# mLSTM stage: eight heads' scores in four PSUM banks at once, gates on four column groups, and the state's product ahead of the scores

## The chip, the cores and the metric

The kernel runs on one core of one Trainium2 chip. Its time is the device time in microseconds, and the number to compare is the median of several executions: 733.33 us here, over three (732.94 to 734.95). One further execution was recorded by the hardware profiler; it took 733.4 us, of which the span from the first to the last instruction is 731.6 us. Every duration below comes from that execution. TensorE (PE) multiplies matrices into PSUM, its weight loads are shown apart as PEld, VectorE is DVE, ScalarE is ACT, GpSimd is POOL, and SyncE (SP) issues most DMAs.

## The reference, cut to what matters

Two transformer-like layers follow each other on x of 4 x 256 tokens with 256 features, in float32: an attention, a gated feed-forward with a Hadamard transform, an mLSTM block with its own gated feed-forward, and a feed-forward with int8 weights. A layer norm stands after each. The part that the change touches is the mLSTM, with 8 heads of 16 query and key features and 32 value features:

```
i = cap(h @ w_ig + b_ig); f = cap(h @ w_fg + b_fg)      # two gates per head and token, cap = 15*tanh(x/15)
F = cumsum(log_sigmoid(f)); D[s,t] = F[s] - F[t] + i[t]  for t <= s, else -inf
m = max_t D;  C = (q k^T / 4) * exp(D - m)
out = (C @ v) / max(|sum_t C|, exp(-m)), then a norm per head, and sigmoid(o) times it
x1 = x + out @ w_out ;  then rmsnorm and silu(x1 w_gate) * (x1 w_up) @ w_down
```

The kernel splits a sequence of 256 tokens in two blocks of 128. Within a block it forms the scores directly; the second block gets what the first one left from a state, the sum of k v^T over the first block, multiplied by q.

## The kernel before

The tokens are cut in two halves `n` = 0 and 1, each of 512 tokens, which are two sequences `bb`. After the attention (to about 434 us) the feed-forward of half 0 runs, then the mLSTM of half 0 while the feed-forward of half 1 (`ffn0(1)`) fills in, then the feed-forward that belongs to the mLSTM (`ffn1(0)`), and with it the mLSTM of half 1; then `ffn1(1)` and the int8 feed-forward.

`mlstm(n)` is a Python generator. Each number that it yields is a wait in microseconds that its author reckons with; `merge(first, other)` (L958) advances the filling stream by about that much matmul work before it goes on. The filling stream yields 1.7 after each of its 512-column products in `glu` (L543) and after each half of a `down` product (L557). This makes the program's order; the build then fixes one order of instructions for each engine, which may move an instruction ahead of others that have to wait. Each engine works through its own list in that order.

For one half the steps are: `mlstm_in` (L613) normalizes the tokens, transposes them to `fm` (L534), multiplies by `w_if` for the gates, by `w_qk` for q and k (L639 f.), and by `w_vo` for v and the output gate, four times (L651). `gates` (L674) is a chain of small ACT and DVE steps on the gate values, which lie on 64 partitions; its running maximum `gmax` goes to DRAM as `far` (L689). `by_token` (L699) transposes three rows of factors to token order (`tok`), and the keys are multiplied out once more by token (`ks`). `within` (L736) handles four heads of one sequence: it loads `far` back, broadcast over 128 partitions, as `wide` (L740), multiplies q and k of four heads in two PSUM banks (L747), subtracts `wide` from a mask on POOL (L756), takes eight exponentials on ACT (L763), and multiplies scores and exponentials on DVE (L767). `between` (L711) forms the state (L714, L719) and its product with q (L726, L729). `attend` (L773) multiplies by the values (L778), one small product per head and block. `head_norm` (L788) is a chain on DVE and ACT that ends in `xs` (L808). Then follow the transposes of `xs` (L534), `w_out` (L850), the addition to `acc` (L851), and in `ffn1` a root mean square norm (L517 to 527), transposes of `h` (L534) and the first product with `w_gate`.

[...] The mLSTM takes its banks in turn from two pairs (`pt`, `ot`), the filling stream from the other two pairs (`mm`, `sc`).

A float32 matmul stands in the trace as two MATMUL records with a weight load each; counts in the profile are therefore twice those in the code. [...]

Of the kernel before, what the change touches and what calls it, by code (L numbers as in the profile page):

```python
# [16 lines left out]
P = 128  # L17
# [21 lines left out]
def tile_two_layers(ctx: ExitStack, tc: tile.TileContext, a: dict, out: bass.AP):  # L39
# [26 lines left out]
    def mm_k(ps, lhs, rhs, n):  # L66

        for i in range(n):
            nc.tensor.matmul(ps, lhsT=lhs(i), rhs=rhs(i), start=(i == 0), stop=(i == n - 1))  # L69


    wts = tc.alloc_tile_pool(name="wts", bufs=1, side="right")
# [394 lines left out]
    w_if = late.tile([P, KC, 64], F32, tag="w_if", name="w_if")  # L467
    nc.gpsimd.memset(w_if, 0.0)
    nc.sync.dma_start(w_if[:, :, 0:40], a["w_if"])
    b_if = late.tile([64, 2], F32, tag="b_if", name="b_if")  # L470
    nc.gpsimd.memset(b_if, 0.0)
    for bb in range(2):
        for g in range(2):
            nc.sync.dma_start(b_if[32 * bb : 32 * bb + H1, g : g + 1], a["b_if"][32 * g : 32 * g + H1, :])
    vecs = load("vecs", [P, 6])
    w_vo = load("w_vo", [P, KC, 2 * D])
    w_qk = late.tile([P, KC, 2, P], F32, tag="w_qk", name="w_qk")
# [51 lines left out]
    def transposed(src, dst, tag, weight=None):  # L529
# [10 lines left out]
                evicted = nc.vector.tensor_scalar(dst[:, c, :], pt, weight[:, c : c + 1], None, ALU.mult)  # L540
        return evicted

    def glu(xT, wg, wu, hT, tag):  # L543

        for c in range(NH):
            cols = slice(c * P, (c + 1) * P)
            pg, pu = bank(tag), bank(tag)
            mm_k(pg, lambda i: wg[:, i, cols], lambda i: xT[:, i, :], KC)
            yield 1.7
            mm_k(pu, lambda i: wu[:, i, cols], lambda i: xT[:, i, :], KC)  # L550
            g = work.tile([P, HALF], F32, tag="glu_g", name="glu_g")
            nc.scalar.activation(g, pg, AF.Tanh, scale=0.5)
            nc.vector.scalar_tensor_tensor(g, g, 1.0, pg, ALU.add, ALU.mult)
            nc.vector.tensor_tensor(hT[:, c, :], pu, g, ALU.mult)
            yield 1.7
# [45 lines left out]

    ones = mix.tile([2 * 32, S], F32, tag="ones", name="ones")
    nc.gpsimd.memset(ones, 1.0)
    bias = mix.tile([2 * 32, 2], F32, tag="bias", name="bias")
    nc.scalar.mul(bias, b_if, 1.0 / CAP)
    DV = DV1 + 1
    HV = H1 * DV
# [5 lines left out]
    def mlstm_in(n, t):  # L613
# [5 lines left out]
        transposed(hin, fm, "m", vecs[:, 0:2])  # L619
        yield 1.7  # L620
        pg = bank("m")
        for g in range(2):
            for bb in range(2):
                mm_k(
                    pg[32 * bb : 32 * bb + 32, g * S : (g + 1) * S],
                    lambda i: w_if[:, i, 32 * g : 32 * g + 32],
                    lambda i: fm[:, i, bb * S : (bb + 1) * S],
                    KC,
                )
        gt = mix.tile([64, 2, S], F32, tag="gt", name="gt")  # L630
        for g in range(2):
            nc.scalar.activation(
                gt[:, g, :], pg[:64, g * S : (g + 1) * S], AF.Tanh,
                bias=bias[:, g : g + 1], scale=1.0 / CAP,
            )
        gates(n, t, gt)
        yield 0.0
        pq, pk = bank("m"), bank("m")
        mm_k(pq, lambda i: w_qk[:, i, 0, :], lambda i: fm[:, i, :], KC)  # L639
        mm_k(pk, lambda i: w_qk[:, i, 1, :], lambda i: fm[:, i, :], KC)  # L640
        qT = mix.tile([P, HALF], F32, tag="qT", name=f"qT{n}")
        nc.scalar.mul(qT, pq, 1.0 / math.sqrt(DQK))
        kT = mix.tile([P, 2, HALF], F32, tag="kT", name=f"kT{n}")
# [2 lines left out]
        va = mix.tile([P, NJH, H1, DV], F32, tag="va", name=f"va{n}")  # L646
        nc.gpsimd.memset(va[:, :, :, DV1], 1.0)
        sig = mix.tile([P, NJH, D], F32, tag="sig", name=f"sig{n}")
        for j in range(NJH):
            pv = bank("m")  # L650
            mm_k(pv, lambda i: fm[:, i, j * P : (j + 1) * P], lambda i: w_vo[:, i, :], KC)  # L651
            nc.scalar.copy(va[:, j, :, 0:DV1], pv[:, 0:D].rearrange("p (h d) -> p h d", h=H1))
            nc.scalar.activation(sig[:, j, :], pv[:, D:], AF.Tanh, scale=0.5)
        t.update(va=va, sig=sig, qT=qT, kT=kT)
        yield 1.0
        by_token(n, t)
        pt = bank("m")
        for bb in range(2):
            mm_k(
# [14 lines left out]
    def gates(n, t, gt):  # L674

        rows = mix.tile([64, 3, S], F32, tag="rows", name="rows")
        g, em, fac = rows[:, 0, :], rows[:, 1, :], rows[:, 2, :]
        lsp = mix.tile([64, S], F32, tag="lsp", name="lsp")
        fcum = mix.tile([64, S], F32, tag="fcum", name="fcum")
        gmax = mix.tile([64, S], F32, tag="gmax", name="gmax")  # L680
        neg = mix.tile([64, 1], F32, tag="neg", name="neg", bufs=2)
        nc.scalar.activation(lsp, gt[:, 1, :], AF.Exp, scale=-CAP)
        nc.scalar.activation(lsp, lsp, AF.Ln, bias=1.0)
        nc.vector.tensor_tensor_scan(fcum, ones, lsp, 0.0, ALU.mult, ALU.subtract)
        nc.vector.scalar_tensor_tensor(g, gt[:, 0, :], CAP, fcum, ALU.mult, ALU.subtract)
        nc.vector.tensor_tensor_scan(gmax, g, g, -3.0e38, ALU.max, ALU.max)
        far = dram.tile([2, H1, S], F32, tag=f"far{n}", name=f"far{n}")
        for bb in range(2):
            nc.sync.dma_start(far[bb], gmax[32 * bb : 32 * bb + H1, :])  # L689
        t["far"] = far  # L690
        last = gmax[:, P - 1 : P]
        nc.vector.tensor_scalar_mul(neg, last, -1.0)
        nc.vector.tensor_tensor(lsp, fcum, gmax, ALU.add)
        nc.scalar.activation(fac[:, 0:P], g[:, 0:P], AF.Exp, bias=neg)
        nc.scalar.activation(fac[:, P:S], gmax[:, P:S], AF.Exp, bias=last, scale=-1.0)
        nc.scalar.activation(em, lsp, AF.Exp, scale=-1.0)
        t["rows"] = rows
# [35 lines left out]
        t["part", bb] = part  # L733
        yield

    def within(t, bb, half):  # L736


        wide = mix.tile([P, HG, S], F32, tag="wide", name="wide", bufs=2)
        nc.sync.dma_start(wide, t["far"][bb, half * HG : (half + 1) * HG].partition_broadcast(P))  # L740
        ps = (bank("m"), bank("m"))
        for odd in range(2):
            for c in range(2):
                for k in range(2):
                    rows = slice(32 * (2 * half + k), 32 * (2 * half + k) + 32)
                    tok = slice(bb * S + c * P, bb * S + (c + 1) * P)
                    nc.tensor.matmul(  # L747
                        ps[k][:, (2 * odd + c) * P : (2 * odd + c + 1) * P],
                        lhsT=t["kT"][rows, odd, tok], rhs=t["qT"][rows, tok],
                        start=True, stop=True,  # L750
                    )
        out = []
        for k in range(2):
            h = 4 * half + 2 * k
            ex = mix.tile([P, 4, P], F32, tag="ex", name="ex", bufs=4)
            nc.gpsimd.tensor_tensor(  # L756
                ex, mask.unsqueeze(1).to_broadcast([P, 4, P]),
                wide[:, 2 * k : 2 * k + 2, :].rearrange("p h (c s) -> p (h c) s", c=2), ALU.subtract,
            )
            for odd in range(2):  # L760
                for c in range(2):
                    at = 32 * bb + h + odd
                    nc.scalar.activation(  # L763
                        ex[:, 2 * odd + c, :], ex[:, 2 * odd + c, :], AF.Exp,
                        bias=t["tok"][:, c, 0, at : at + 1],
                    )
            nc.vector.tensor_tensor(  # L767
                ex, ps[k].rearrange("p (x s) -> p x s", x=4), ex, ALU.mult
            )
            out.append(ex)  # L770
        return out

    def attend(t, bb, half, exs, part, hv):  # L773

        ph = bank("m")
        for c in range(2):
            for x in range(HG):
                nc.tensor.matmul(  # L778
                    ph[:, (c * HG + x) * DV : (c * HG + x + 1) * DV],
                    lhsT=exs[x // 2][:, 2 * (x % 2) + c, :], rhs=t["va"][:, 2 * bb + c, half * HG + x, :],  # L780
                    start=True, stop=True,
                )
        heads = slice(half * HG, (half + 1) * HG)
        by_h = ph[:, : 2 * HG * DV].rearrange("p (c h d) -> p c h d", c=2, h=HG)
        nc.scalar.copy(hv[:, 0, heads, :], by_h[:, 0])
        nc.vector.tensor_tensor(hv[:, 1, heads, :], by_h[:, 1], part[:, heads, :], ALU.add)

    def head_norm(n, t, bb, hv):  # L788

# [23 lines left out]
    def run(stream):  # L813
        for _ in stream:
            pass
# [3 lines left out]

    def mlstm(n):  # L820

        t, waiting = {}, []

        def finish():
            bb, half, exs, hv = waiting.pop()
            attend(t, bb, half, exs, t["part", bb], hv)
            if half == 1:
                head_norm(n, t, bb, hv)

        yield from mlstm_in(n, t)  # L830
        for bb in range(2):
            hv = mix.tile([P, 2, H1, DV], F32, tag="hv", name="hv", bufs=2)
            for half in range(2):
                exs = within(t, bb, half)
                if half == 0:
                    carried = between(t, bb)
                run(take(1, carried))
                yield 1.5
                if waiting:
                    finish()  # L840
                waiting.append((bb, half, exs, hv))
        yield 3.0
        finish()
        yield 6.0
        fm = feature_major(n)
        transposed(hos[n], fm, "m", vecs[:, 2:4])
        yield 1.7
# [272 lines left out]
```

## Time and profile before

| what | value |
|---|---|
| median of three executions | 733.33 us (732.94 to 734.95) |
| profiled execution: time, span | 733.4 us, 731.6 us |
| PE busy | 719.2 us, 98% of the span |
| DVE, ACT, POOL busy | 406.8, 242.2, 179.6 us |
| half 0, from its transposes of `hin` to the first `w_gate` product | 488.9 to 556.0 us |
| half 1, from its transposes of `hin` to the first product of `ffn1(1)` | 567.3 to 634.5 us |
| granted TensorE clock, mean | 0.998 |

In the listings of groups a row reads: line, engine, operation, result and operands, shapes, count, busy time, mean of one. In the timeline a row reads: start, length, engine, line, operation, names, shapes, count, and in brackets the idle time before it with what ended it. Ends of matmuls are modelled by the profiler, so starts of neighbours tell more than lengths.

### The profile page before, as it was taken

Reading aid. Unit: us, or ns where it says so; the run is one execution under the profiler, and the core shown is the slowest. Engines: PE = TensorE matmul, PEld = TensorE weight load, DVE = VectorE, ACT = ScalarE, POOL = GpSimd, SP = SyncE. Lnnn points to the kernel's source line nnn. Section 1 sums busy time; section 2 is a strip of 40 time slices with the busy share of each in tenths; the row PEclk is TensorE's granted clock in tenths of the full one; section 3 lists DMA queues with packets and bytes.
Section 4 is the critical chain, followed back from the end, with each engine's and each line's share of the span. In section 5 each row is a group of like instructions: output and inputs, shape, how many; then the busy total and the mean of one; then the engine's idle time right before and its main releaser. Section 6 shows DMA issues by size and latency. Waiting matters only on the chain.

```text
span 731.6 us, 8898 instructions
## 1 busy us (share of the span) xinstructions
PE 719.2 (98%) x3084; PEld 491.0 (67%) x3084; DVE 406.8 (56%) x1063; ACT 242.2 (33%) x651; POOL 179.6 (25%) x197
## 2 busy tenths in 40 slices
PE   8999999999999999999999999999999999999996
PEld 4657667667767766766776864745775476747995
DVE  0363545555564364455445464374778458844797
ACT  2232432342242243233224331126411461111563
POOL 1721431449441242144044000002200050000221
PEclk9999999999999999999999999999999999999999
DMA  7542143173223222421311322002030110000001
GB/s 233 226 115 55 21 113 59 31 272 58 39 91 58 52 86 52 93 59 37 72 37 22 58 70 56 1 0 87 31 115 1 56 61 1 0 1 0 2 16 43
DMA packets 48108, 45.36 MB, mean 62 GB/s; under 512 B 9504, under 2 KB 42688, under 8 KB 46016
## 3 DMA queue, kind: packets, MB, share of 16 engines
q1 hardware_dynamic: 46928, 40.47, 21.1%
q0 software_dynamic: 432, 3.15, 1.2%
q10 hardware_dynamic: 704, 1.18, 0.5%
q8 instruction: 24, 0.39, 0.3%
q14 instruction: 20, 0.16, 0.1%
HBM read 25.61 MB, written 1.08 MB: 36 GB/s over the span
## 4 chain that ended last, share of the span: by engine, by line
PE 88%; DVE 6%; DMA 2%; ACT 1%; issue 1%; POOL 0%; DVEq 0%; SPq 0%; ACTq 0%; POOLq 0%
PE ps_mm L69 37%; PE ps_d L69 11%; PE ps_ot L69 8%; PE ps_m L69 6%; PE ps_d L561 5%; PE ps_pt L232 4%; PE ps_sc L232 4%; PE ps_sc L241 2%; PE ps_d L861 2%; PE ps_m L561 2%; PE ps_m L778 2%; PE ps_pt L241 2%; DMA wide<-far 1%; PE ps_m L909 1%; DVE gq L891 1%; DMA w_qkv<-in_w_qkv 1%
## 5 line engine op out<-in xcount | busy, mean ns | idle before, releaser
L69 PE MATMUL ps_mm<-xT,w_qkv 128*128 128x512 f32 x248 | 115.7, 593 | 0.0
L176 POOL TENSOR_TENSOR rope_raw<-rope_raw,cst 128x512 f32<-128x512 f32 x32 | 40.7, 1271 | 229.8 <-DVE rope_swp L173 229.8
L260 ACT ACTIVATE pr<-ps_sc,nmax 128x256 f32<-128x256 f32 x64 | 29.5, 472 | 142.2 <-DVE nmax L251 142.2
L69 PEld LDWEIGHTS ps_mm<-xT,w_qkv 128*128 128x128 f32 x248 | 47.0, 190 | 37.2 <-issue 33.8
L69 PEld LDWEIGHTS ps_ot<-prT,v 128*128 128x128 f32 x240 | 45.6, 190 | 28.8 <-issue 25.3
L69 PE MATMUL ps_ot<-prT,v 128*128 128x256 f32 x240 | 60.8, 379 | 0.0
L69 PE MATMUL ps_mm<-w_o,oT 128*128 128x256 f32 x256 | 60.6, 380 | 0.0
L270 DVE TENSOR_SCALAR pr<-pr,rinv 128x256 f32<-128x256 f32 x128 | 58.1, 487 | 1.8
L69 PE MATMUL ps_mm<-xT,w_rot 128*128 128x512 f32 x128 | 59.0, 604 | 0.0
L69 PE MATMUL ps_mm<-w_qkv,xT 128*128 128x256 f32 x256 | 58.1, 379 | 0.6 <-ACT kn L198 0.6
L69 PEld LDWEIGHTS ps_mm<-w_o,oT 128*128 128x128 f32 x256 | 48.4, 190 | 12.9 <-issue 6.0
L69 PE MATMUL ps_d<-fm,w 128*128 128x512 f32 x128 | 56.7, 594 | 0.3 <-ACT fm L538 0.3
L69 PEld LDWEIGHTS ps_mm<-w_qkv,xT 128*128 128x128 f32 x256 | 48.6, 190 | 8.4 <-ACT kn L198 1.0
L251 DVE TENSOR_REDUCE nmax<-ps_sc 128x2 f32<-128x512 f32 x32 | 20.6, 686 | 59.1 <-PE ps_sc L241 59.1
L756 POOL TENSOR_TENSOR ex<-cst,wide 128x512 f32<-128x512 f32 x16 | 19.9, 1265 | 131.8 <-DMA wide<-far 119.4
L210 DVE COPY v<-ps_mm 128x512 f32<-128x512 f32 x32 | 22.0, 691 | 50.4 <-PE ps_mm L69 46.8
L268 DVE RECIPROCAL rinv<-rsum 128x2 f32<-128x2 f32 x64 | 9.7, 152 | 64.3 <-ACT pr L260 64.1
L278 DVE STREAM_TRANSPOSE cross<-pr 128x512 f32<-128x512 f32 x60 | 42.7, 711 | 1.5
L69 PEld LDWEIGHTS ps_d<-fm,w 128*128 128x128 f32 x128 | 24.0, 190 | 27.1 <-issue 24.9
L69 PEld LDWEIGHTS ps_mm<-xT,w_rot 128*128 128x128 f32 x128 | 23.2, 189 | 28.1 <-issue 20.4
L177 POOL TENSOR_TENSOR rope_swp<-rope_swp,cst 128x512 f32<-128x512 f32 x32 | 40.8, 1274 | 0.0
L857 POOL TENSOR_TENSOR qh<-gq,qh 128x256 fp32r<-128x256 f32 x16 | 12.3, 766 | 108.8 <-issue 79.6
(199 smaller groups left out, 1227.5 us busy)
## 6 DMA issues: line engine op xcount, KB each, us to landing
prT<-cross SPq DMA_DIRECT2D x240, 64.0 KB, 2.1
w_qkv<-in_w_qkv SPq DMA_DIRECT2D x7, 1024.0 KB, 5.2
wide<-far SPq DMA_DIRECT2D x8, 512.0 KB, 4.0
w<-in_w SPq DMA_DIRECT2D x3, 1024.0 KB, 13.7
w_o<-in_w_o SPq DMA_DIRECT2D x8, 256.0 KB, 3.1
acc<-in_x SPq DMA_DIRECT2D x2, 512.0 KB
w_gate<-in_w_gate SPq DMA_DIRECT2D x1, 1024.0 KB, 8.7
w_up<-in_w_up SPq DMA_DIRECT2D x1, 1024.0 KB, 10.6
```

What stands on the lines that cost most here:

```text
L69: nc.tensor.matmul(ps, lhsT=lhs(i), rhs=rhs(i), start=(i == 0), stop=(i == n - 1))
L176: nc.gpsimd.tensor_tensor(by_b(raw), by_b(raw), cs, ALU.mult)
L177: nc.gpsimd.tensor_tensor(by_b(swp), by_b(swp), sn, ALU.mult)
L210: return nc.vector.tensor_copy(v[:, 2 * jj : 2 * jj + 2, :], ps.rearrange("p (t d) -> p t d", t=2))
L232: nc.tensor.matmul(ps[bb][e][:, qt * S : (qt + 1) * S], lhsT=qn[:, e, queries(bb, qt)], rhs=kn[:, e, keys(bb)], start=(qt == 0), stop=Fals ...
L241: nc.tensor.matmul(ps[bb][e][:, qt * S : (qt + 1) * S], lhsT=qr[rows, queries(bb, qt)], rhs=kr[rows, keys(bb)], start=False, stop=(qt == 1 ...
L251: nc.vector.tensor_reduce(nmax, ps.rearrange("p (t k) -> p t k", t=2), AX.X, ALU.max, negate=True)
L260: nc.scalar.activation(pr[:, qt, :], ps[:, qt * S : (qt + 1) * S], AF.Exp, bias=nmax[:, qt : qt + 1], accum_out=rsum[:, qt : qt + 1],)
L270: nc.vector.tensor_scalar(pr[:, qt, :], pr[:, qt, :], rinv[:, qt : qt + 1], None, ALU.mult)
L278: return nc.vector.transpose(cross[:, :, e], pr.rearrange("p t (x i) -> p x t i", i=32))
L561: nc.tensor.matmul(po, lhsT=hT[:, i, j * P : (j + 1) * P], rhs=wd[:, i, :], start=(i == 0), stop=(i == NH - 1))
L756: nc.gpsimd.tensor_tensor(ex, mask.unsqueeze(1).to_broadcast([P, 4, P]), wide[:, 2 * k : 2 * k + 2, :].rearrange("p h (c s) -> p (h c) s", ...
```

## The change

1. Gates. The two gates are put below each other on four column groups (partitions 0, 32, 64, 96) of one 256-column stretch, and the loop over the two feature chunks is outermost. One `Tanh` on 128 partitions takes the place of two on 64. The q and k products are ordered behind the last gate product.
2. `distances` is new: directly after `gates`, for both sequences of the half, it loads `far` broadcast into a tile `ex` for all eight heads, and subtracts in place on POOL. `decays` takes the exponentials in place on ACT, in portions of eight, ordered behind the latest `Tanh` of `glu`.
3. `by_token` and the keys by token stand before the fourth v-o product, not after it.
4. `mlstm` is reordered: for each sequence the state, a filling wait of 2.5, its product with q, a wait of 2.5, then `within` for all eight heads in four banks (four row groups in turn), a wait of 3.4, and `attend` for both sets of four heads. The waits at the end are 1.5 and 7.5, where they were 3.0 and 6.0.

The number of matmuls, DMAs and exponentials is unchanged; two `Tanh` instructions are saved.

```diff
-        for g in range(2):
-            for bb in range(2):
-                mm_k(
-                    pg[32 * bb : 32 * bb + 32, g * S : (g + 1) * S], ...
+        for i in range(KC):
+            for g in range(2):
+                for bb in range(2):
+                    at = 64 * g + 32 * bb
+                    gated = nc.tensor.matmul(
+                        pg[at : at + 32, 0:S], lhsT=w_if[:, i, 32 * g : 32 * g + 32],
+                        rhs=fm[:, i, bb * S : (bb + 1) * S], start=(i == 0), stop=(i == KC - 1),
+                        skip_group_check=True,
+                    )
+        gt = mix.tile([P, S], F32, tag="gt", name="gt")
+        nc.scalar.activation(gt, pg[:, 0:S], AF.Tanh, bias=bias, scale=1.0 / CAP)
         gates(n, t, gt)
+        for bb in range(2):
+            distances(t, bb)
...
+        with tc.issue_after(gated.ins):
+            mm_k(pq, lambda i: w_qk[:, i, 0, :], lambda i: fm[:, i, :], KC)
+            mm_k(pk, lambda i: w_qk[:, i, 1, :], lambda i: fm[:, i, :], KC)
...
         for j in range(NJH):
+            if j == NJH - 1:
+                by_token(n, t)
+                keys_by_token(n, t, fm)
             pv = bank("m")
...
+    def distances(t, bb):
+        ex = mix.tile([P, H1, 2, P], F32, tag="ex", name="ex", bufs=2)
+        for half in range(2):
+            heads = slice(half * HG, (half + 1) * HG)
+            nc.sync.dma_start(
+                ex[:, heads].rearrange("p h c s -> p h (c s)"), t["far"][bb, heads].partition_broadcast(P)
+            )
+        for r in range(HG):
+            two = ex[:, 2 * r : 2 * r + 2].rearrange("p h c s -> p (h c) s")
+            nc.gpsimd.tensor_tensor(
+                two, mask.unsqueeze(1).to_broadcast([P, 4, P]), two, ALU.subtract
+            )
+        t["ex", bb] = ex
+
+    def decays(t, bb, half):
+        ex = t["ex", bb]
+        with tc.issue_after(evictions[-1].ins):
+            for h in range(half * HG, (half + 1) * HG):
+                for c in range(2):
+                    at = 32 * bb + h
+                    nc.scalar.activation(
+                        ex[:, h, c, :], ex[:, h, c, :], AF.Exp, bias=t["tok"][:, c, 0, at : at + 1]
+                    )
...
-    def within(t, bb, half):
-        ps = (bank("m"), bank("m"))
+    def within(t, bb):
+        ps = [bank("m") for _ in range(HG)]
         for odd in range(2):
             for c in range(2):
-                for k in range(2):
-                    rows = slice(32 * (2 * half + k), 32 * (2 * half + k) + 32)
+                for r in range(HG):
+                    rows = slice(32 * r, 32 * r + 32)
...
         yield from mlstm_in(n, t)
         for bb in range(2):
             hv = mix.tile([P, 2, H1, DV], F32, tag="hv", name="hv", bufs=2)
+            for k, _ in enumerate(between(t, bb)):
+                yield 2.5
+                if not bb and not k:
+                    decays(t, 0, 1)
+            within(t, bb)
+            if not bb:
+                decays(t, 1, 0)
+            yield 3.4
             for half in range(2):
-                exs = within(t, bb, half)
-                if half == 0:
-                    carried = between(t, bb)
-                run(take(1, carried))
+                attend(t, bb, half, hv)
+            if not bb:
+                decays(t, 1, 1)
                 yield 1.5
-                if waiting:
-                    finish()
-                waiting.append((bb, half, exs, hv))
-        yield 3.0
-        finish()
-        yield 6.0
+            head_norm(n, t, bb, hv)
+        yield 7.5
```

The order of TensorE's matmuls that the build gives the changed kernel for half 0, from the gates on (counts as in the code, to be doubled for the trace; "fill" is work of `ffn0(1)`):

```
w_if 8, w_qk 4, w_vo 6, transposes of rows 6, keys by token 4, w_vo 2,
state 1, fill 512-col 2, state x q 1, fill 512-col 4, scores 16, fill 512-col 4, attend 16, fill 512-col 2,
state 1, fill 512-col 2, state x q 1, fill 512-col 4, scores 16, fill down 8, attend 16, fill down 16,
transposes of xs 8, fill down 4, w_out 8, fill down 4, transposes of h 8, w_gate ...
```

In the kernel before, the end of the same list reads: attend 8, fill 512-col 6, transposes of xs 4, fill down 9, transposes of xs 4, fill down 2, w_out 8, fill down 10, transposes of h 8, fill down 11, w_gate. Half 1 has the same order as half 0 up to `w_out`, with `down` of `ffn1(0)` as its fill. After `w_out` the kernel before has 21 down matmuls and then the transposes of `h`; the changed kernel has 4 down matmuls, four transposes for the int8 feed-forward, the transposes of `h` and three matmuls of the int8 feed-forward.

## The prediction

> **What bounds the kernel now.** First the page: busy times, and the shares of the chain that ended last.
>
> ```profile
> PE 719.2 (98%) x3084; PEld 491.0 (67%) x3084; DVE 406.8 (56%) x1063; ACT 242.2 (33%) x651; POOL 179.6 (25%) x197
> PE 88%; DVE 6%; DMA 2%; ACT 1%; issue 1%; POOL 0%; DVEq 0%; SPq 0%; ACTq 0%; POOLq 0%
> ```
>
> TensorE sets the end, with 12 us idle in all. So I look only for matmul time that goes and for idle time that comes. Next, the timeline of PE over the mLSTM of half 0 (start, length, line, names, count):
>
> ```profile
> 491.24 0.62 PE L69 MATMUL ps_m<-fm,w_if 128*32 128x256 f32 x2
> 491.79 1.13 PE L69 MATMUL ps_m<-fm,w_qk 128*128 128x512 f32 x2
> 492.85 1.92 PE L69 MATMUL ps_m<-fm,w_if 128*32 128x256 f32 x14
> 494.70 2.84 PE L69 MATMUL ps_m<-fm,w_qk 128*128 128x512 f32 x6
> 497.38 7.03 PE L69 MATMUL ps_m<-w_vo,fm 128*128 128x512 f32 x16
> ...
> 505.94 1.16 PE L747 MATMUL ps_m<-qT,kT 32*128 32x128 f32 x16
> 507.03 0.71 PE L714 MATMUL ps_m<-va,ks 128*128 128x264 f32 x2
> 507.58 1.88 PE L69 MATMUL ps_d<-fm,w 128*128 128x512 f32 x4
> 509.39 1.49 PE L747 MATMUL ps_m<-qT,kT 32*128 32x128 f32 x16
> 511.06 0.68 PE L726 MATMUL ps_m<-state,qT 128*128 128x264 f32 x2 [0.18 <-DVE ex L767]
> 511.58 1.88 PE L69 MATMUL ps_d<-fm,w 128*128 128x512 f32 x4
> ...
> 541.82 3.69 PE L69 MATMUL ps_m<-w_out,fm 128*128 128x256 f32 x16
> 545.35 4.48 PE L561 MATMUL ps_d<-w,hT 128*128 128x256 f32 x20
> 549.87 1.55 PE L534 MATMUL ps_d<-cst,h 128*128 128x128 f32 x8
> 551.26 4.91 PE L561 MATMUL ps_d<-w,hT 128*128 128x256 f32 x22
> 556.01 1.88 PE L69 MATMUL ps_d<-fm,w_gate 128*128 128x512 f32 x4
> ```
>
> Between 491.24 and 497.38 stand eight q and k records, 8 x 0.429 = 3.43, so the sixteen gate records and their changes of shape take 2.7. One set of sixteen score records takes 1.09 from its start to the next start, the second 1.67, since it waits for a bank. After `w_out` there are 20 and then 22 records of filling work around the transposes of `h`: they hide the norm. Third, the chain of waits over the same stretch:
>
> ```profile
> 500.77 1.31 DMA far<-gmax
> 502.10 4.14 DMA wide<-far
> 506.32 1.27 POOL ex L756
> 507.61 2.52 ACT ex L763 x8
> ```
>
> From `gmax` (500.74) to the multiplication of scores that frees a bank for the product at 511.06 pass 10 us, the one wait that TensorE shows here, of 0.2 us.
>
> [...] `w_if` starts 0.52 after the 512-column record before it, not 0.43, and the record after it shows its weight load of 0.1. So about 0.2 per switch. [...] The trace shows two groups at work: score records alternate, a pair every 0.105 us, where one alone takes 0.107. Four are not in it.
>
> **The change part by part,** for one half.
>
> *Gates.* Sixteen records over four column groups are four in a row, 4 x 0.215 = 0.86; with two switches and the wait for the second chunk of `fm` some 1.1. Against 2.7: saves 1.6. If only two groups overlap, 0.9 of that is lost.
>
> *Scores.* A set of sixteen costs its 1.09 and the 0.2 of the switch into it; four are 5.2, and the second waits besides. After: two sets of 32 over four row groups, 8 x 0.107 = 0.86, with the switches 1.25 each, 2.5. Saves 2.7 without the wait. If only two groups overlap, 0.86 is lost again per set.
>
> *One `Tanh`, moved factors.* The gate chain starts when the gates end, at about 492.4 and not 494.8, and its `Ln` no longer stands behind the copy of q. `gmax` comes at 497.5, not 500.74. So the transposes of the rows, now ahead of the fourth v-o product (at 501.1), find their rows (499.3). Cost nothing; the slack is 1.8.
>
> *DMAs, POOL, exponentials.* SP issues two `far` and, directly behind, four loads of 512 KB: no other DMA stands behind them there. Landing after 1.31 + 4.14 (rows above) gives 503.0 for the first. Four in flight instead of two may be slower; I lay the next at 1.2 each. POOL, 1.27 each, is done with sequence 0 at 508.0 and with sequence 1 at 513. ACT, 0.313 per exponential by the starts, ends sequence 0's sixteen at about 509.5; ahead of it wait only the last v and gate copies, whose bank the scores need at 510.5. Scores end at 511.7, the four multiplications (0.61 apart) at 514.4, `attend` comes at 515.0. Hidden, by 0.6 of the multiplications and two to three microseconds of the loads; beyond that every microsecond late is one on TensorE.
>
> *Filling work moved ahead.* Here the gain is lost. By the end of the last `attend` the changed order has spent 12 more records of 512 columns and 16 of down, 8.6 us of fill, so this end comes at 534.6, not 530.7 (8.6 - 4.6 saved). What is left as cover is 32 down records, 6.9 us, to 541.5. `head_norm` took from 530.7 to 540.27, with four multiplications of `glu` beside it on DVE; I take 1.3 less without them: `xs` at 542.9, and TensorE waits about 1. `w_out` then runs from 545.2 to 548.7, and 8 down records to 550.4. From the end of `w_out` to the transposes of `h` the old trace has 4.5 (545.35 to 549.87), all under fill; the same 4.6 now ends at 553.3: idle 2.9. After these transposes (1.0) the first copy of `fm` on DVE, 0.7 with its waits, is bare too: idle 0.8. So `w_gate` comes at about 555.3, not 556.0.
>
> *Sum.* I laid the lists of all engines end to end with the durations of the rows. Half 0: 4.6 saved on TensorE (gates 1.6 to 1.7, scores 2.7 and a little of the wait), idle 4.7 where the old order has some 0.6 in the same places: 0.6 gained. Half 1: idle 4.0, as four transposes and three matmuls of the int8 part stand in its gaps, and its `hin` isn't late: 1.0. These matmuls are then done: 0.3. Together 1.9. Not in it are the waits for a bank by which the old second score set exceeds my layout, 0.3 in half 0 and 0.5 in half 1; they go, and I count 0.7: 2.6. The profiled span of 731.6 becomes 729.0. Its execution took 733.4, 1.8 more than the span, and the median of 733.33 agrees: forecast 730.7.
>
> **Rivals.**
>
> *A. The groups don't overlap four at a time* (slower). The issue of small matmuls, or weight loads on four groups, sets their pace at that of two. For it: the trace shows no more than two. Against: the pairs start 5 to 7 ns apart, so issue isn't near its limit[...]. Price: 4 score sets x 0.86 + 2 x 0.86 at the gates = 5.2, all ahead of the chain that ends a half: 730.7 + 5.2 = 735.9. It decides from a set of 32 taking more than 1.9 us.
>
> *B. The idle gaps lower the clock* (no gain or slower). In the trace the clock fell to half 3.5 us after the last matmul (724.7 to 728.2). The gap here is 2.9, then transposes, then 0.8. [...]
>
> *C. The saved matmul time counts in full.* The chain after `attend` is shorter than I think, as DVE has less beside it: 2 x 4.6 = 9.2, less at least the bare copies, 2 x 0.8: 733.3 - 7.6 = 725.7. Against: in the old trace the second transposes of `xs` (540.33) already came straight from `xs`, with no slack.
>
> *D. Nothing is gained.* The chain is 1 us longer per half than laid out: the loads of `ex` contend, or the fill's layer norm is in its way. 733.
>
> **How the numbers follow.** The main case 0.62, 729.3 to 732.5; A 0.08, B 0.08, C 0.10, D 0.12. A measurement of this kernel can tell about 0.3%, 2.2 us, from no change, so "faster" means below 731.1: of the main case two thirds (0.42) and all of C, 0.52. Same: 0.20 of the main case, D, half of B: 0.36. Slower: A and half of B, 0.12. The range runs from between C and the main case, 728.3, to just above B in both halves, 734.8; it leaves out most of C and of A.
>
> **What would show it.** Right: sixteen `w_if` records in about 1.1 us; 32 score records within 1.3 us, in fours; PE idle of 2 to 3 us before the transposes of `h` in both halves, put down to DVE, and about 1 before those of `xs`; PE busy less by some 9 us; the first multiplication of scores waiting for PE, not for ACT or POOL. Wrong: waits of `attend` for `ex` (the loads), a clock below 1.00 after 550 or 625, score sets near 2 us, or no idle at `h`.

## The result, and the profile after

The changed kernel takes 738.7 us (median of six executions, 737.5 to 740.0) against 734.07 for the kernel before, measured beside it: ratio 1.0066, interval 1.0053 to 1.0079. It is slower by 0.66%, where the forecast was 730.7 and the range ended at 734.8. The profiled execution took 737.5 us with a span of 735.4. Its mean granted clock is 0.986, that of before 0.998. All six executions show 0.986.

First the page of the kernel after: busy times, and the shares of the chain that ended last.

```profile
PE 717.5 (98%) x3084; PEld 491.0 (67%) x3084; DVE 404.0 (55%) x1063; ACT 241.1 (33%) x649; POOL 179.3 (24%) x197
PE 91%; DVE 7%; ACT 1%; DMA 1%; issue 0%; ACTq 0%
```

TensorE's busy time fell by 1.7 us only, where the same products in faster sets should have made it about 9 less. So some products became slower. The timeline of PE over half 0 says which (start, length, engine, line, names, count; the line numbers are those of the kernel after):

```profile
490.62 1.07 PE L630 MATMUL ps_m<-fm,w_if 128*32 128x256 f32 x16
491.63 3.70 PE L69 MATMUL ps_m<-fm,w_qk 128*128 128x512 f32 x8
...
509.77 1.17 PE L780 MATMUL ps_m<-qT,kT 32*128 32x128 f32 x32
510.87 3.70 PE L69 MATMUL ps_d<-fm,w 128*128 128x512 f32 x8
...
530.49 4.22 PE L796 MATMUL ps_m<-va,ex 128*128 128x33 f32 x32
534.52 9.96 PE L565 MATMUL ps_d<-w,hT 128*128 128x256 f32 x32
...
547.46 3.62 PE L69 MATMUL ps_m<-w_out,fm 128*128 128x256 f32 x16
550.91 1.89 PE L565 MATMUL ps_d<-w,hT 128*128 128x256 f32 x8
555.54 1.23 PE L536 MATMUL ps_d<-cst,h 128*128 128x128 f32 x8 [2.75 <-DVE h L527]
557.51 3.55 PE L69 MATMUL ps_d<-fm,w_gate 128*128 128x512 f32 x4 [0.73 <-DVE fm L542]
```

The gates take 1.01 from their start to the next start, a set of 32 score records 1.10: both as meant. By the trace the records start in fours, 6 to 7 ns from one to the next within a four; behind the first, the fours of scores follow 0.11 us apart and those of the gates 0.22. The idle time ahead of the transposes of `h` is 2.75, near the 2.9 that was reckoned. What is new are two lengths. Four records of `w_gate` took 3.55 where such a four took 1.88 in the kernel before, and 32 records of `down` took 9.96 where eight still take 1.89 a little later. The table by stretches tells why (stretch, busy us and count of PE, PEld, DVE, ACT and POOL, granted clock, DMA share, GB/s):

```profile
529.92:533.33 3.41, 3.41 (x31) 3.33 (x29) 1.46 (x5) 0.27 (x1) 0.00 (x0) 1.00 0.30 103
533.33:536.75 3.42, 3.42 (x13) 3.02 (x13) 1.33 (x4) 0.50 (x2) 0.15 (x1) 0.51 0.00 0
536.75:540.16 3.41, 3.41 (x9) 2.70 (x8) 1.12 (x4) 0.63 (x1) 0.00 (x0) 0.50 0.00 0
550.40:553.81 3.41, 2.40 (x12) 1.76 (x10) 2.23 (x11) 1.02 (x4) 0.00 (x0) 1.00 0.00 0
553.81:557.22 3.41, 1.23 (x8) 0.81 (x8) 3.22 (x21) 0.00 (x0) 0.00 (x0) 1.00 0.00 0
557.22:560.63 3.41, 3.12 (x4) 1.51 (x5) 3.41 (x14) 0.00 (x0) 0.00 (x0) 0.51 0.02 5
```

The clock is at half (0.50 or 0.51) in 533.33 to 540.16 and in 557.22 to 560.63. In half 1 it is so (0.51) in 615.2 to 618.7 and in 635.7 to 639.1. That is 17.1 us at half the clock, up to 8.5 us of lost matmul time; the kernel before has none until 3.5 us after its last product (at 728.2). Each stretch is 3.41 us or twice that, and all starts lie whole multiples of 3.413 apart (557.22 - 533.33 = 7 x 3.413; by the trace 533.39, 557.29, 615.32 and 635.79, the last two 24 and 30 times 3.413 behind the first). So in this execution the clock changed on a grid of 3.41 us only; below, a window is one piece of that grid. In each half one stretch follows the window with the bare gap (1.23 us busy of 3.41 in half 0). The other follows a window in which TensorE had no idle time at all: 529.92 to 533.33 is busy for 3.41, of which 2.84 with `attend` records.

So the theory to test has two parts: the bare gap at `h` dropped the clock here, and so did the run of 32 small `attend` records (3.5 us) that the change makes out of two runs of sixteen. In the kernel before, these two runs stood apart:

```profile
523.61 1.87 PE L778 MATMUL ps_m<-va,ex 128*128 128x33 f32 x16
525.31 3.68 PE L69 MATMUL ps_d<-fm,w 128*128 128x512 f32 x8
528.83 1.87 PE L778 MATMUL ps_m<-va,ex 128*128 128x33 f32 x16
```

The rivals: the clock is incidental, and the loss is in the order of the filling work and the chain on VectorE; or the sets on four row or column groups pull the clock down.

### The profile page after: what moved, and what is told of

Same layout as the page of the kernel before. It is cut to its first block, busy times and chain, and to the rows that moved or that the text cites. A ratio compares the mean times of both kernels' runs of the same rounds, so it can differ in the third digit from the quotient of the medians.

```text
span 735.4 us, 8884 instructions
## 1 busy us (share of the span) xinstructions
PE 717.5 (98%) x3084; PEld 491.0 (67%) x3084; DVE 404.0 (55%) x1063; ACT 241.1 (33%) x649; POOL 179.3 (24%) x197
## 4 chain that ended last, share of the span: by engine, by line
PE 91%; DVE 7%; ACT 1%; DMA 1%; issue 0%; ACTq 0%
PE ps_mm L69 37%; PE ps_d L69 12%; PE ps_m L69 8%; PE ps_ot L69 8%; PE ps_d L565 5%; PE ps_pt L233 4%; PE ps_sc L233 4%; PE ps_sc L242 2%; PE ps_m L796 2%; PE ps_d L876 2%; PE ps_m L565 2%; PE ps_pt L242 2%; PE ps_m L924 1%; DVE gq L906 1%; PE ps_m L536 1%; DMA w_qkv<-in_w_qkv 1%
## 5 line engine op out<-in xcount | busy, mean ns | idle before, releaser
L755 POOL TENSOR_TENSOR ex<-cst,ex 128x512 f32<-128x512 f32 x16 | 19.7, 1262 | 117.2 <-DMA ex<-far 117.2
```

What stands on the lines that cost most here:

```text
L755: nc.gpsimd.tensor_tensor(two, mask.unsqueeze(1).to_broadcast([P, 4, P]), two, ALU.subtract)
```

## The experiments

**Fill the gap.** Six matmul records of constants are put into the idle time; nothing is reordered.

```
 def transposed(src, dst, tag, weight=None, idle=0):
     for c in range(KC):
         pt = bank(tag)
+        for _ in range(idle if c == 0 else 0):
+            nc.tensor.matmul(pt, lhsT=ident, rhs=w_vo[:, 0, :], start=True, stop=True)
...
-    evicted = transposed(h2, fm, tag, vecs[:, 4:6])
+    evicted = transposed(h2, fm, tag, vecs[:, 4:6], idle=3)
```

> Added work only: three 128x512 products of constants (six records, 2.6 us) into the bank of the transposes of `h`, straight ahead of them, in both halves. Nothing is reordered; the idle time of 2.75 and 2.31 us there is filled. Clock theory: the half-clock stretches at 557.2 to 560.6 and 635.7 to 639.1 go (mean granted clock from 0.986 to about 0.991), which gives back about 1.6 us each, less 0.3 in half 1 where the added products are longer than the gap: 735.8 us. If the clock is incidental and the chain on VectorE is the loss: 738.7 to 739.3, clock as it may be. If the four-group tiles pull the clock down: the stretches stay, 739.

Measured: 734.3 us (before beside it 733.88), ratio 1.0003, interval 0.9991 to 1.0015; 4.4 below the changed kernel, where 2.9 were expected. Added work made the kernel faster. The table by stretches of this kernel:

```profile
530.40:533.90 3.50, 3.50 (x33) 3.49 (x32) 1.24 (x4) 0.27 (x1) 0.00 (x0) 1.00 0.21 70
534.10:537.40 3.30, 3.30 (x9) 2.59 (x9) 1.93 (x5) 1.13 (x3) 0.15 (x1) 0.50 0.00 0
553.80:557.20 3.40, 2.78 (x11) 1.58 (x12) 3.31 (x13) 0.00 (x0) 0.00 (x0) 1.00 0.00 0
557.20:560.60 3.40, 3.40 (x9) 1.52 (x8) 3.28 (x11) 2.19 (x9) 0.00 (x0) 1.00 0.02 5
```

The stretch behind the transposes of `h` is gone, in both halves (1.00 from 557.20 to 560.60, and from 635.6 to 639.0). The one behind the last `attend` is still there, in half 0 now one window long (3.41) where it was two. Nothing ahead of it differs, so that is put down to where the windows fell; half of the 3.41 us of that window, 1.7, would account for the 1.5 beyond the 2.9. The chain on VectorE is as long as before:

```profile
549.16 1.89 PE L567 MATMUL ps_d<-w,hT 128*128 128x256 f32 x8
550.89 2.74 PE L536 MATMUL ps_d<-w_vo,cst 128*128 128x512 f32 x6
553.79 1.40 PE L538 MATMUL ps_d<-cst,h 128*128 128x128 f32 x8 [0.17 <-DVE h L527]
```

From the `down` records to the transposes of `h` it takes 4.63, as in the changed kernel (550.91 to 555.54). So the loss at `h` was the clock.

**Break the run of `attend`**, in two ways. Once with an added product of constants between the two blocks of sequence 1:

```
 def attend(t, bb, half, hv):
     ph = bank("m")
+    if bb and half:
+        nc.tensor.matmul(ph, lhsT=ident, rhs=w_vo[:, 0, :], start=True, stop=True)
```

> Added work only: one 128x512 product of constants (two records, 0.86 us) between the two `attend` blocks of sequence 1 in both halves, so that its 32 small records are no longer in one run. Clock theory: the half-clock stretches at 533.3 to 540.2 and 615.2 to 618.7 go; about 4 us come back, and the added product costs up to 0.86 in each half since the chain after `attend` sets the end: 736.4 us, clock about 0.992; the stretches at `h` stay. If the clock is incidental: 739.6 to 740.4. If the four-group tiles pull the clock down: stretches stay, 740.4.

And once with the filling work that stands there anyway:

```
-            yield 3.4
             for half in range(2):
+                yield 1.7
                 attend(t, bb, half, hv)
```

> No added work: the 3.4 us of filling work between scores and `attend` is dealt out as 1.7 before each of the two `attend` blocks. Clock theory: the stretches after the last `attend` go (clock about 0.992), the last `attend` still ends with the same fill spent, so 734.7 us. If the clock is incidental: 738.7.

Measured: 734.24 for the dealt filling work (ratio 1.0007, 0.9996 to 1.0018), 738.98 for the added product (735.0 to 739.9; ratio 1.0059, 1.0036 to 1.0082). In the first, the stretches behind the last `attend` are gone, those at `h` stay, here that of half 0 (in half 1 it is 634.5 to 637.9, at 0.50), as the clock theory says:

```profile
530.90:536.10 5.20, 5.20 (x42) 4.99 (x40) 2.48 (x6) 0.27 (x1) 0.00 (x0) 1.00 0.48 173
536.10:539.50 3.40, 3.40 (x18) 3.01 (x18) 1.95 (x6) 1.13 (x3) 0.16 (x1) 1.00 0.00 0
556.00:559.40 3.40, 2.90 (x4) 1.35 (x5) 3.40 (x14) 0.00 (x0) 0.00 (x0) 0.50 0.02 5
```

The second missed its 736.4. In its profile too the stretches behind sequence 1 are gone. But one stands now behind the unbroken run of sequence 0 in half 1, and the one at `h` in half 0 lasts two windows:

```profile
597.10:600.50 3.40, 3.40 (x32) 3.38 (x31) 0.99 (x2) 1.71 (x6) 0.00 (x0) 1.00 0.02 5
600.50:603.90 3.40, 3.40 (x7) 1.68 (x7) 1.42 (x4) 0.50 (x2) 0.00 (x0) 0.51 0.00 0
```

With the stretch at `h` in half 1 that is four windows at half the clock, one fewer than in the changed kernel; what that gives back, 1.7, the two added products cost (0.86 each). Sequence 0's run had been there in the changed kernel and done no harm. There, by the grid, the border between two windows fell inside it (at 598.25, in a run from 595.95 to 599.44; in half 0 at 516.3, in a run from 514.4 to 517.9). In these two profiles the run of 32 was hit where 2.9 us of it or more lay in one window, and spared where a border cut it to 2.3 us or less. The six executions of the kernel with the added product have clocks of 0.988 to 0.993, so not every one of them has the same falls.

**Both additions.**

> Both additions together. Clock theory: no half-clock stretch before the end, clock about 0.998, and 738.7 - 3.2 - 4 + 2 = 733.5 us. If the clock is incidental: 740.7.

Measured: 732.7 us (732.0 to 739.4 over 14 executions), ratio 0.9997, interval 0.998 to 1.0014. That is 6 us faster than the changed kernel with more work in it, and no chain on VectorE was touched: the theory of an incidental clock, 740.7, falls. Ten executions have a clock of 0.998 or 0.999 and take 732.0 to 733.9; the other four have 0.989 to 0.996 and take 735.5 to 739.4. The profiled one is of the latter, and shows sequence 0 of half 1 once more:

```profile
594.00:597.40 3.40, 3.40 (x31) 3.16 (x29) 1.08 (x3) 1.98 (x7) 0.00 (x0) 1.00 0.00 0
597.40:600.80 3.40, 3.40 (x8) 1.85 (x8) 1.41 (x4) 0.50 (x2) 0.00 (x0) 0.51 0.00 0
```

**The prediction's layout without the clock.** The dealt filling work (which parts the blocks of both sequences) and the filled gap, together.

> The changed kernel with both remedies that leave its order of filling work alone: the two `attend` blocks of every sequence apart by 1.7 us of the filling work, and three added 128x512 products of constants in the gap ahead of the transposes of `h`. This is the layout that the prediction laid end to end, without the fall of the clock: clock 0.998, and 730.7 us plus up to 0.3 for the added products in half 1, so 731.0. If the layout was wrong by more than the clock took: 733 or more.

Measured: 730.88 us, ratio 0.9962, interval 0.9948 to 0.9976, with a clock of 0.997 or 0.998 in every execution. So the layout of the prediction, but for where `attend` stands and with the gap filled, is worth 3.5 us against before (734.39 beside it). The falls of the clock cost about 738.7 - 730.9 = 7.8 us.

**The run of small products alone, in the kernel before.** Nothing of the change is in this kernel; only the `attend` of sequence 1's first four heads waits for the last.

```
-            bb, half, exs, hv = waiting.pop()
+            bb, half, exs, hv = waiting.pop(0)
...
-                if waiting:
+                if waiting and not (bb and half):
                     finish()
...
         yield 3.0
         finish()
+        finish()
```

> The kernel before with one thing moved: the `attend` of sequence 1's first four heads waits and runs back to back with that of its last four, so that 32 small records stand in one run of 3.5 us, as after. No column or row group of the change is in it, no idle gap is made, and the last `attend` comes no later. Clock theory: in executions whose 3.41-us windows fall mostly inside the run a half-clock stretch of 3.41 us follows it, at a price of up to 1.7 us in each half: clock 0.993 to 0.998, median about 735.6 us between 733.9 and 737.3. If a run of small products is harmless and the idle gaps or the groups are what does it: 733.9, clock 0.998 throughout.

Measured: 734.86 us (732.5 to 736.9 over 22 executions) against 733.23, ratio 1.0019, interval 1.0009 to 1.003. The expected median was 0.7 too high, but the fall came. Sixteen of the 22 executions have a clock of 0.993 to 0.995 and take 734.2 to 736.9. Of the six with 0.997 or 0.999, four take 732.5 to 732.6, but two 734.9 and 736.5, so not every slower execution is one with a fall. The timeline of PE and the table by stretches, in the profiled execution:

```profile
527.21 3.65 PE L778 MATMUL ps_m<-va,ex 128*128 128x33 f32 x32
```

```profile
527.40:530.80 3.40, 3.40 (x32) 3.40 (x32) 3.16 (x11) 0.86 (x2) 0.00 (x0) 1.00 0.02 5
530.80:534.20 3.40, 3.40 (x6) 1.32 (x6) 0.69 (x3) 0.50 (x2) 0.16 (x1) 0.51 0.01 2
```

A window filled with the 32 records, TensorE busy for 3.40 of 3.40 us and no wait ahead of it, is followed by one at half the clock (0.51). In half 1 of the same execution the same run (from 607.7) lies across the border of two windows, and the clock stays at 1.00 (607.7 to 614.5). With the kernel before otherwise as it was, neither a gap nor a set on four groups was needed for the fall.

**One part alone: the gates** on four column groups with one `Tanh`, in the order of before.

```
-        for g in range(2):
-            for bb in range(2):
-                mm_k(
-                    pg[32 * bb : 32 * bb + 32, g * S : (g + 1) * S],
-                    lambda i: w_if[:, i, 32 * g : 32 * g + 32],
-                    lambda i: fm[:, i, bb * S : (bb + 1) * S],
-                    KC,
-                )
+        for i in range(KC):
+            for g in range(2):
+                for bb in range(2):
+                    at = 64 * g + 32 * bb
+                    nc.tensor.matmul(
+                        pg[at : at + 32, 0:S], lhsT=w_if[:, i, 32 * g : 32 * g + 32],
+                        rhs=fm[:, i, bb * S : (bb + 1) * S], start=(i == 0), stop=(i == KC - 1),
+                        skip_group_check=True,
+                    )
...
+        nc.scalar.activation(gt, pg[:, 0:S], AF.Tanh, bias=bias, scale=1.0 / CAP)
```

> The kernel before with one part of the change alone: the gates on four column groups and one `Tanh`. The order of filling work stays that of before, so the tail of each half keeps its cover. Clock theory: sixteen gate records in about 1.0 us where the old order took 2.7, no half-clock stretch before the end (clock 0.998), and the whole saving counts: 733.9 - 2 x 1.6 = 730.7 us. If the tiled sets pull the clock down: a half-clock stretch near 494 and 575, 734 to 736. If the four column groups don't really pay, only the record times shrink: 733.9.

Measured: 728.53 us, ratio 0.9933, interval 0.9919 to 0.9947, clock 0.997 to 0.999: 4.7 us faster than before, 10 faster than the whole change. The rival that tiled sets pull the clock down falls, for the column groups. The timeline of PE shows the saving, and more beyond the 1.6 a half that was expected:

```profile
491.70 1.07 PE L627 MATMUL ps_m<-fm,w_if 128*32 128x256 f32 x16
...
508.25 1.16 PE L745 MATMUL ps_m<-qT,kT 32*128 32x128 f32 x16
509.34 0.71 PE L724 MATMUL ps_m<-state,qT 128*128 128x264 f32 x2
```

The gates take 1.00 where they took 2.7. The second score set takes 1.09 to the next start, where it took 1.67 before (1.87 in half 1): the chain from `gmax` to the bank that it waits for now starts earlier (`gmax` is done at 498.0 and not at 500.7). 2 x 1.7 + 0.6 + 0.8 = 4.8, and 4.7 was measured.

**The whole change with its filling work dealt out again.** If the order is what makes the gap and the run, another order should keep the gain. No work is added or left out.

```
+    FILL = ((2.1, 1.7), (1.7, 0.0))
...
             for k, _ in enumerate(between(t, bb)):
-                yield 2.5
+                yield FILL[bb][k]
...
-            yield 3.4
-            for half in range(2):
-                attend(t, bb, half, hv)
+            yield 1.7
+            attend(t, bb, 0, hv)
+            yield 1.7
+            attend(t, bb, 1, hv)
...
-                yield 1.5
-        yield 7.5
+        yield 8.5
...
-    merge(chain(take(1, one), [6.0]), other)
+    merge(chain(take(1, one), [5.1]), other)
     run(take(1, one))
     run(other)
...
-    merge(chain(take(1, one), [6.0]), left)
+    merge(chain(take(1, one), [5.1]), left)
+    run(take(1, one))
     run(left)
     run(one)
```

> The changed kernel with its filling work dealt out again, none added or left out: one unit of 1.7 us after the state's product and after the first product with q, one ahead of each `attend` block, none elsewhere in the middle; so ten units instead of seven are left once the last `attend` is done: five for the chain to `xs`, one for the copies of `fm`, three between `w_out` and the transposes of `h`, one behind these. Clock theory: no run of small records and no idle gap near a window long, so clock 0.998, and the 4.6 us a half that matmul time got shorter count, less some 0.5 of idle time a half: 733.9 - 9.2 + 1.0 = 725.7 us. If the tail on VectorE is what the change lost by, and can't be covered: idle of 2 to 3 us a half stays, 729 to 731. If the loads of `ex`, POOL or the exponentials are late for scores that now come 3.4 us earlier: `attend` waits 1 to 2 us a half, 728.

Measured: 734.28 us (730.7 to 739.7 over 22 executions), ratio 1.0014, interval 0.9996 to 1.0032. That missed 725.7 by far. The tail has no idle time any more: `h` and `fm` are covered. But the first `attend` waits 2.4 us in half 0 and 1.8 in half 1, and in half 0 of the profiled execution the clock falls behind it (0.50 from 518.1 to 521.5). The times spread with the clock: nine executions at 0.995 take 730.7 to 733.2, six at 0.983 to 0.986 take 737.3 to 739.7. The timeline of ACT, DVE and PE shows the queue:

```profile
507.61 5.94 ACT L767 ACTIVATE ex<-ex,tok 128x128 f32<-128x128 f32 x20
513.45 0.58 ACT L556 ACTIVATE glu_g<-ps_d 128x512 f32<-128x512 f32 x1
...
514.06 0.69 DVE L557 SCALAR_TENSOR_TENSOR glu_g<-glu_g,ps_d 128x512 f32<-128x512 f32 x1 [5.17 <-ACT glu_g L556]
514.66 2.48 DVE L787 TENSOR_TENSOR ex<-ps_m,ex 128x512 f32<-128x512 f32 x4
515.40 2.19 PE L796 MATMUL ps_m<-va,ex 128*128 128x33 f32 x16 [2.40 <-DVE ex L787]
```

Twenty exponentials, of which only the first twelve were for the scores at hand, stood ahead of the `Tanh` of a filling unit. DVE's list held that unit's step ahead of the multiplications of scores, so these started at 514.66 and not at about 511.0, where the scores end. It was one of the rivals (late exponentials), by a way through two queues that it hadn't named.

**The same with these exponentials behind the first `attend` block**, and a variant with one unit of filling work more ahead of the scores of sequence 0 (its `FILL` is `((2.1, 3.4), (1.7, 0.0))`).

```
-            if not bb:
-                decays(t, 1, 0)
             yield 1.7
             attend(t, bb, 0, hv)
+            if not bb:
+                decays(t, 1, 0)
```

> The last kernel with one thing moved: the exponentials of sequence 1 are issued behind the first `attend` block of sequence 0 and no longer ahead of it, so that the `Tanh` of a filling unit, and behind it on VectorE the four multiplications of scores, no longer wait for them. If the two idle gaps ahead of the first `attend` (2.4 and 1.8 us) were that queue, they go, and with them the half-clock stretch that followed: clock 0.998, PE idle under 1 us from 490 to 640, 733.2 - 9.2 + 1.0 = 725.0 us. If it is the loads or POOL that come late, the gaps stay: 730 or more.

> As that one, but one unit of filling work more (1.7 us) stands between the first product with q and the scores of sequence 0, and one less behind the transposes of `h`. If the exponentials are no longer late in the other kernel, this one only uncovers the copies of `fm` behind the transposes of `h`, 0.7 us a half, too short to touch the clock: 726.5 us, clock 0.998. If the other kernel still waits for its exponentials, this one is the faster: about 727 against 730.

Measured: 726.6 us (four executions), ratio 0.9904, interval 0.9886 to 0.9921, and 727.59 (five), ratio 0.9909, 0.9892 to 0.9925. Both have a clock of 0.997 to 0.999 in every execution. The idle time ahead of `attend` is gone, so it was that queue. In the timeline of PE of the first, after (and not with) filling work:

```profile
508.14 1.17 PE L780 MATMUL ps_m<-qT,kT 32*128 32x128 f32 x32
509.25 1.98 PE L69 MATMUL ps_d<-fm,w 128*128 128x512 f32 x4
511.06 2.13 PE L796 MATMUL ps_m<-va,ex 128*128 128x33 f32 x16
...
519.31 1.90 PE L780 MATMUL ps_m<-qT,kT 32*128 32x128 f32 x32
521.14 1.98 PE L69 MATMUL ps_d<-fm,w 128*128 128x512 f32 x4
```

No row between 490 and 640 has a wait ahead of it. One is hidden inside the second score set of each half, though, which takes 1.83 to the next start where the first takes 1.11. It stands directly behind the product with q, whose bank VectorE empties (`part`, 519.58 to 520.00), and by the trace 22 of its 32 records start only after that, from 520.06 on. These 0.7 us a half are most of what is missing to the expected 725.0. This first kernel has all the parts of the change and beats both: 7.9 us below the kernel before (734.53 beside it), 12 below the changed one. The score sets on four row groups stand in it without a fall of the clock (0.997 or 0.998 in all four executions). The variant bares 0.41 ahead of `w_gate` in half 0 and 0.9 in all at `attend`, and no clock falls (0.998 or 0.999). The two intervals overlap, so whether the one unit matters can't be said.

## Why the prediction was wrong

*Gates and scores: right.* 1.01 us for the gates where 1.1 was reckoned; 1.10 for a set of 32 scores where 1.25 was. Rival A, that the groups don't overlap four at a time, is out: it needed 1.9. 32 records in 1.10 are 0.034 each, where the sets of sixteen took 0.068 (1.09): the fours follow each other at 0.112, as the pairs did before (the prediction's 0.105 runs from the second of one pair to the first of the next).

*Loads, POOL, exponentials hidden: right in this order.* No `attend` waits for them. How thin the cover was shows in the first kernel with all its filling work dealt out again.

*Idle times: right.* In half 0 2.75 at `h` (2.9 reckoned), 0.73 at `w_gate` (0.8). At `xs` 0.31 instead of 1; with the clock whole (the kernels with both remedies) it is 0.56.

*The sum: right, for a clock that stays.* 2.6 gained was the sum, 3.5 came in the kernel that keeps the layout and the clock. That its 730.88 lies so near to the forecast of 730.7 is in part luck: the kernel before stood at 733.33 when the forecast was made and at 734.39 beside that run.

*The clock: the step that failed.* The sum counted every product at the full clock and so put the clock at nothing; it stood only in rival B, at a chance of 0.08. The runs show 17.1 us at half the clock instead, at a cost of about 7.8. B named a cause, idle time, its place at `h`, and a sign, a clock below 1.00 after 550 or 625, that came. Three things in it were wrong. First its chance: the prediction's own idle times and the transposes between them (2.9, 1.0, 0.8) are together longer than the 3.41 us of a window, and in all six halves that were profiled with the gap bare (the changed kernel and both ways of breaking the run) the clock fell there: to 0.51 in the changed kernel, to 0.50 in the one with the dealt filling work and in half 0 of the one with the added product, in whose half 1 four `w_gate` records took 2.61 for 1.88. The gap was weighed too lightly: of the window that it left, TensorE was busy for only 1.23 us of 3.41 in half 0 of the changed kernel and 1.09 of 3.40 in half 1. Second, it looked for idle time alone. The change to two `attend` blocks in one run was counted as a move without cost, and made the other half of the stretches. Third, the range ended just above what B reckoned for both halves (734.8); there were five windows.

*Rivals C and D.* C, that the saved time counts in full (725.7), is false for this order; with the filling work dealt out as in the last kernels it is nearly what happens (726.6). D's 1 us of a longer chain isn't seen.

In the changed kernel a gap of 2.75 us, with transposes and 0.73 more behind it, was enough for half the clock (0.51 from 557.22 to 560.63), and so was a window without any (529.92 to 533.33, busy for all of its 3.41 us, with 0.51 behind it).

## What to carry to other kernels

The clock fell here behind runs of 32 small products (3.5 us) and behind gaps of 2.3 to 2.75 us. When a change gathers such a run or bares such a gap, look at how much of a whole 3.41-us window, the grid of these profiles, is left to wide products (256 or 512 columns here), and put filling work between the pieces: dealing out the same work again, with one set of exponentials moved, was worth 12 us here, more than the 9.2 us of matmul time (2 x 4.6) that the prediction had the change save. A product of constants in a gap can pay, too: three in each half ahead of the transposes of `h` made the kernel 4.4 us faster than the changed one. And try each part of a change alone: the gates alone gained 4.7 us that the whole change hid.

## What had not been expected of the hardware

A busy TensorE lost its clock behind small products: busy for 3.40 of 3.40 us, then at 0.51 (the run alone in the kernel before). An `attend` record has 33 columns and takes 0.109 us (3.5 / 32), where a 512-column one takes 0.429; at that one's pace 33 columns would be 0.028 us, a quarter of the record's time. An estimate from that: count wide products in full, `attend` by a quarter, idle time as nothing. Then the windows full of `attend` that were followed by half the clock hold between 0.25 (nothing but `attend`) and 0.36 by this count: at the last `attend` of the changed kernel in half 0, 0.51 us of wide products and a quarter of 2.90, with the window's end at 533.39, where the clock fell. A window with 0.61 us of wide products and 2.80 of `attend` (sequence 0 in half 1 of the kernel with the filled gap, 592.08 to 595.49 by the grid of its two stretches), 0.38, was not followed by one. That is a border read from a few windows, not one that a run was made to find.

One bare gap doesn't fit this estimate, if a transpose counts in full. In two kernels two windows have nearly the same busy time, and only the first is followed by half the clock. It is that at `h` in half 1 of the kernel that parts the `attend` blocks, with eight transposes (0.98 us) and three 256-column products:

```profile
631.08:634.50 3.42, 1.58 (x11) 1.19 (x11) 3.23 (x21) 0.13 (x1) 0.00 (x0) 1.00 0.01 2
634.50:637.91 3.41, 3.06 (x4) 1.51 (x5) 3.29 (x13) 0.00 (x0) 0.00 (x0) 0.50 0.00 0
```

The other is ahead of the first `attend` in half 1 of the first kernel with all its filling work dealt out again, with hardly anything but 512-column products:

```profile
589.78:593.20 3.42, 1.57 (x5) 0.47 (x3) 1.43 (x3) 3.42 (x13) 2.37 (x2) 1.00 0.00 0
593.20:596.61 3.41, 3.35 (x20) 2.55 (x21) 2.54 (x5) 1.14 (x4) 0.00 (x0) 1.00 0.02 7
```

So in this pair the busy time of TensorE (1.58 and 1.57 us) doesn't tell which is followed by half the clock. The eight transposes stand in the first; that they are the cause was not shown. It is one pair of windows; no run was made to test it.

In the changed kernel the clock came back after one window at 0.51 that was filled with wide products (615.2 to 618.7, from 615.7 on with `down` alone). It took a second window, to 540.16, where the first 1.2 us of the one at half (533.33 to 536.75) were the end of the run of `attend`. But in the first kernel with all its filling work dealt out again a window at half the clock (0.50) also held 1.2 us of `attend` (518.1 to 521.5), and the clock came back. What decides there stays open.

Open too: at the same clock, the times of the changed kernel lie in two groups, 737.5 to 737.9 and 739.5 to 740.0, and so do those of the kernel before, 732.9 to 733.3 and 734.8 to 735.3. No run here tells what parts them.
